# Room for routed rows by rank, and the ranks' room looked up with a matmul

## The chip, the cores and the metric

The kernel runs on one core of a Trainium2 chip. The metric is device time in microseconds (us), the median over runs of the whole kernel. Engines: TensorE (PE; PEld is its weight load), VectorE (DVE), ScalarE (ACT), GpSimd (POOL) and SyncE (SP), which issues most DMAs.

## The reference

One transformer layer in float32 on x of 2 x 1024 tokens by 256 channels: a layer norm and grouped attention (16 heads, 4 key/value heads, head size 16, rotary positions), added to x; then a layer norm and a mixture of experts, added as well. What matters here is the second half, for 2048 tokens:

```python
shared = silu(gu[:, :704]) * gu[:, 704:] @ se_down_w.T * sigmoid(x @ shared_gate_w.T)
probs = softmax(x @ gate_w.T)               # 60 experts
weights, sel = top_k(probs, 4)
for e in range(60):                          # w13[e]: 352 x 256, w2[e]: 256 x 176
    h = silu(x @ w13[e].T[:, :176]) * (x @ w13[e].T[:, 176:])
    sparse += cw[:, e, None] * (h @ w2[e].T)
out = x + shared + sparse
```

Only four experts of sixty have a weight for a token, so 8192 rows (token, expert) need an expert's work, about 137 each and unevenly spread.

## The kernel before, in words

Stages, in order of time: attention over 128 steps (0 to about 360 us), in the gaps of which tokens are routed; the first half of the shared expert, on which the end of routing is laid (to about 418 us); the routed experts (to about 614 us); the second half of the shared expert, on which the gathers of the routed results are laid; the output.

**Routing** (`route`) finds each token's four experts and a slot for each. Tokens go to DRAM (`xg`) by indirect DMA (L739): each expert has 2048 slots there, of which the first `CAP` = 208 were filled at the start with empty rows (L163). An empty row carries the token number `NONE` = 1e6, so its result is dropped by the bounds check of the scatter back.

**Ranks.** The program is fixed before the counts are known. So `count` and `ranks` order the experts by their number of rows on the chip, and the program's r-th expert is whichever has rank r; its number is read into a register from `byrank` (L810, L972). The list `CAPS` gives the room, in rows, with which rank r is worked on: 208 for 6 ranks, 192 for 4, 176 for 8, 160 for 10, 144 for 8, 128 for 24, together 9,248. `ranks` makes `slotid` (L813, L818: slot numbers of the first and second tile of each rank) and `caps` (L824 to L832: the room of each expert, built up in five steps of two operations). From `caps` and the counts comes `nblk` (L847): how many blocks of 128 rows lie beyond an expert's room. If any does (L1278), a loop over all 60 experts works off the rest, block by block (`over_block`).

**The expert stage.** Rooms over 128 are worked in two tiles of half the room each, others in one tile (`tile_of`, L1164). For each rank in the order `turn_of` (L959, which spreads the sizes evenly):

- `bring` loads 624 KB of weights into one of eight buffers (L984), `rows_of` loads the rows from `xg` (L1172), both on SP's queue;
- `turned` transposes the rows on PE (L1182, one per tile and half of the channels) and DVE copies the result to `xT` (L1188);
- `up` has six matmuls on PE with as many columns as the room (L917), SiLU on ACT (L924, L926) and products on DVE (L925, L927) into `hbuf`;
- `second` lets `place` (L947) compute where each row's result goes (`dst`, L952 and L956 on DVE), multiplies by the second weights (L1200: two matmuls of 256 columns for each tile), copies on ACT (`ys`, L1207) and scatters from POOL (L933, one indirect DMA for each tile).

The order on every engine of this stage but POOL is written out by hand: `up` of expert k, `turned` of k+2, `second` of k-1, then the row load of k+4 and the weight load of k+7. In the shared expert's first half the order is also by hand: after each step of matmuls (L863, L885) a piece of routing or ranking follows.

Of the kernel before, what the change touches and what calls it, by code (L numbers as in the profile page):

```python
# [8 lines left out]
F32 = mybir.dt.float32  # L9
# [3 lines left out]
ALU = mybir.AluOpType  # L13
# [3 lines left out]
P = 128  # L17
# [8 lines left out]
E, I = 60, 176  # L26
# [7 lines left out]
FB = 512  # L34
RB = 4

CAPS = [208] * 6 + [192] * 4 + [176] * 8 + [160] * 10 + [144] * 8 + [128] * 24
CAP = max(CAPS)
SP = CAP // 2
ES = NT * P  # L40
OB = -(-(ES - min(CAPS)) // P)
SLT, TOK = C, C + TOPK
XA = 4
WA = 8
XR = C + 16
# [2 lines left out]
NONE = 1e6  # L48
# [3 lines left out]
def attention_moe_kernel(  # L52
# [9 lines left out]
    ws2: bass.AP,  # L62
    rope: bass.AP,
    odd: bass.AP,
    tri: bass.AP,
    out: bass.AP,
):
    nc = tc.nc
# [9 lines left out]
    const = ctx.enter_context(tc.tile_pool(name="const", bufs=1, side="left"))  # L78
# [5 lines left out]
    ident = const.tile([P, P], F32, name="ident")  # L84
# [5 lines left out]
    xg = dram.tile([E * ES + 2 * P, XR], F32, name="xg")  # L90
# [47 lines left out]
    wout_sb = ends_of.tile([P, G // 2, C], F32, name="wout_sb")  # L138
    nc.sync.dma_start(wout_sb, wout)
    nc.sync.dma_start(wgate_sb, wgate.rearrange("(c p) n -> p c n", p=P))  # L140
    tri_sb = const.tile([P, P], F32, name="tri_sb")
    nc.sync.dma_start(tri_sb, tri)
    for a, b in ((RB, TPB), (TPB, NT)):
        nc.sync.dma_start(
            xT_sb[:, :, a * P : b * P], xtr[:, a * P : b * P].rearrange("(c p) n -> p c n", p=P)
        )
        nc.sync.dma_start(acc[:, a:b, :], xt[:, a:b, :])
# [13 lines left out]
    for e in range(E):  # L161
        rows = xg[e * ES : e * ES + CAP, :].rearrange("(t p) c -> p t c", p=SP)
# [3 lines left out]
    for i in range(TOPK * NT // 2):  # L166
        rows = yt[2 * i * P : 2 * (i + 1) * P, :].rearrange("(t p) c -> p t c", p=P)
# [4 lines left out]
    slotid = const.tile([P, E, 2], F32, name="slotid")  # L172
    keyrow = const.tile([P, E], F32, name="keyrow")
    keycol = const.tile([E, 1], F32, name="keycol")
    down = const.tile([E, E], F32, name="down")
    expno = const.tile([E, P], F32, name="expno")
    slot1 = const.tile([P, 1], F32, name="slot1")
    rowno = const.tile([P, OB], F32, name="rowno")
    kplace = const.tile([P, TOPK], F32, name="kplace")
    tokno = const.tile([P, NT], F32, name="tokno")  # L180
    for t, pattern, first, by_row in (

        (base, [[ES, E]], 1, 0),

        (keyrow, [[-1, E]], E, 0),
        (keycol, [[0, 1]], E, -1),
        (down, [[-1, E]], E - 1, 0),
        (expno, [[0, P]], 0, 1),
        (slot1, [[0, 1]], 1, 1),
        (rowno, [[P, OB]], 0, 1),  # L190
        (kplace, [[NT * P, TOPK]], 0, 0),
        (tokno, [[P, NT]], 0, 1),
    ):
        nc.gpsimd.iota(
            t,
            pattern,
            base=first,
            channel_multiplier=by_row,
            allow_small_or_imprecise_dtypes=True,
        )  # L200
    tri_b = const.tile([P, P], BF16, name="tri_b")
    nc.gpsimd.tensor_copy(tri_b, tri_sb)
    ones_b = const.tile([P, P], BF16, name="ones_b")
    nc.gpsimd.memset(ones_b, 1.0)
    ones_f = const.tile([E, P], F32, name="ones_f")
# [17 lines left out]
    start = const.tile([P, E], F32, name="start")  # L223
# [579 lines left out]
    def ranks(bank):  # L803

        who = bank(2 * E, "who")
        nc.tensor.matmul(who[:, 0:E], lhsT=expno, rhs=key["has"], start=True, stop=True)
        nc.tensor.matmul(
            who[:, E : 2 * E], lhsT=ones_f[0:E, :], rhs=key["ahead_of"], start=True, stop=True
        )
        nc.vector.tensor_copy(byrank, who[0:1, 0:E])  # L810
        rank = rk.tile([P, E], F32, name="rank")
        nc.vector.tensor_copy(rank, who[:, E : 2 * E])
        nc.vector.tensor_scalar(slotid[:, :, 0], who[:, 0:E], ES, slot1, ALU.mult, ALU.add)  # L813
        r0 = 0
        for cap in sorted(set(CAPS), reverse=True):
            r1 = r0 + CAPS.count(cap)
            if cap > P:
                nc.vector.tensor_scalar_add(  # L818
                    slotid[:, r0:r1, 1], slotid[:, r0:r1, 0], cap // 2
                )  # L820
            r0 = r1
        yield
        caps = rk.tile([P, E], F32, name="caps")
        nc.vector.memset(caps, float(min(CAPS)))  # L824
        for r in range(1, E):
            if CAPS[r] < CAPS[r - 1]:

                step = rk.tile([P, E], F32, name=f"step{r}")
                nc.vector.tensor_scalar(
                    step, rank, r - 0.5, CAPS[r - 1] - CAPS[r], ALU.is_lt, ALU.mult  # L830
                )
                nc.vector.tensor_add(caps, caps, step)  # L832
        yield
        nc.vector.tensor_sub(over, cnt, caps)
        nc.vector.tensor_add(start, caps, base)
        nc.vector.tensor_copy(cap0, caps[0:1, :])
        more = rk.tile([1, E, OB], F32, name="more_b")
        nc.vector.tensor_tensor(
            more,
            over[0:1, :, None].to_broadcast([1, E, OB]),  # L840
            rowno[0:1, None, :].to_broadcast([1, E, OB]),
            ALU.is_gt,
        )
        blks = rk.tile([1, E + 1], F32, name="blks")
        nc.vector.tensor_reduce(blks[:, 0:E], more, AX.X, ALU.add)
        nc.vector.tensor_reduce(blks[:, E : E + 1], blks[:, 0:E], AX.X, ALU.max)
        nc.vector.tensor_copy(nblk, blks)  # L847
# [96 lines left out]
        tc.add_to_no_dep_group("back", s.ins)  # L944
        scattered.append(s)

    def place(dst, rows, me):  # L947

        n = rows.shape[0]
        k0 = small.tile([n, 1], F32, tag="k0", name="k0")  # L950
        hit = small.tile([n, TOPK], F32, tag="wh", name="wh")
        nc.vector.scalar_tensor_tensor(  # L952
            hit, rows[:, SLT : SLT + TOPK], me, kplace[0:n, :], ALU.is_equal, ALU.mult,
            accum_out=k0,
        )
        nc.vector.tensor_add(dst, k0, rows[:, TOK : TOK + 1])  # L956


    turn_of = [  # L959
        r for _, r in sorted(  # L960
            ((k + 0.5) / CAPS.count(cap), CAPS.index(cap) + k)
            for cap in set(CAPS)
            for k in range(CAPS.count(cap))
        )
    ]
    ws = []
# [29 lines left out]
    with tc.manual_schedule(engines={mybir.EngineType.PE}), ExitStack() as both:  # L996
# [17 lines left out]
        behind = [(0, late)]  # L1014
# [148 lines left out]

        def tile_of(cap):  # L1164

            return (cap // 2, 2) if cap > P else (cap, 1)

        def rows_of(r):
            rows, n = tile_of(CAPS[r])
            no = expert_at(r)  # L1170
            xe = ew.tile([P, 2, XR], F32, tag="xe", bufs=XA + 3, name=f"xe{r}")[0:rows, 0:n, :]
            nc.sync.dma_start(  # L1172
                xe, xg[bass.ds(no * ES, CAPS[r]), :].rearrange("(t p) c -> p t c", p=rows)
            )
            return xe

        def turned(r, xe):
            rows, n = tile_of(CAPS[r])
            tp = ps_x.tile([P, CC, CAP], F32, tag="tpe", name=f"tpe{r}")[:, :, 0 : CAPS[r]]
            for t in range(n):  # L1180
                for c in range(CC):
                    nc.tensor.transpose(  # L1182
                        tp[:, c, t * rows : (t + 1) * rows],
                        xe[:, t, c * P : (c + 1) * P],
                        ident[0:rows, 0:rows],
                    )
            xT = ew.tile([P, CC, CAP], F32, tag="xT", name=f"xT{r}")[:, :, 0 : CAPS[r]]
            nc.vector.tensor_copy(xT, tp)  # L1188
            return xT

        def second(r, w, h, xe):
            rows, n = tile_of(CAPS[r])
            dst = ew.tile([P, 2], I32, tag="dst", name=f"dst{r}")[0:rows, :]
            for t in range(n):
                place(dst[:, t : t + 1], xe[:, t, :], slotid[0:rows, r, t : t + 1])
            po = ps_y.tile([P, 2, C], F32, tag="ye", name=f"ye{r}")[0:rows, 0:n, :]
            ys = ew.tile([P, 2, C], F32, tag="ys", name=f"ys{r}")[0:rows, 0:n, :]
            for t in range(n):
                for k in range(2):
                    nc.tensor.matmul(  # L1200
                        po[:, t, :],
                        lhsT=h[:, k, t * rows : (t + 1) * rows],
                        rhs=w[:, CC * W1C + k * C : CC * W1C + (k + 1) * C],
                        start=k == 0,
                        stop=k == 1,
                    )
            nc.scalar.copy(ys, po)  # L1207
            for t in range(n):
                send_back(ys[:, t, :], dst[:, t : t + 1])
# [113 lines left out]
def _laid_out(inputs):  # L1323
# [20 lines left out]
    for m in range(NC2):  # L1344
# [10 lines left out]
    rope = np.concatenate([cos, cos, -sin, sin], 1).astype(np.float32)  # L1355
    q = a["q_kernel"].reshape(C, NKV, G // 2, 2 * H).transpose(0, 2, 1, 3).reshape(C, NH * H)
    wout = a["out_kernel"].reshape(NKV, G // 2, 2 * H, C).transpose(0, 2, 1, 3)
    return {
        "x": a["x"],
        "xtr": a["x"].reshape(B * T, C).T,  # L1360
# [5 lines left out]
        "ws2": ws2,  # L1366
        "rope": rope.reshape(TPB, P, 2 * H).transpose(1, 0, 2),
        "odd": (np.arange(P) // H % 2).astype(np.int32)[:, None],
        "tri": np.triu(np.ones((P, P), np.float32), 1),
    }  # L1370


# [20 lines left out]
```

## Time and profile before

| | us |
|---|---|
| median of 3 runs (677.0 to 678.4) | 678.12 |
| the profiled execution | 678.74 |
| its span, first to last instruction | 676.9 |
| PE busy in the span | 663.9 |
| first row transpose of the expert stage, start | 417.85 |
| last pass of the expert stage, end | 613.22 |
| first matmul after it (L863), start | 614.55 |
| last matmul (L885), end | 673.3 |

A row of the profile names the line, the engine, the operation and its tiles, out<-in, with the shape and the number of instructions. A busy PE is not a PE at its peak, since matmuls are pipelined; the spacing of their starts says more than the length of one. A wait names the engine and line that waited, then the one that ended the wait, then total us, times and the longest.

### The profile page before, as it was taken

What the parts mean: (1) busy time and instruction counts of PE and PEld (TensorE: products, weight loads), DVE (VectorE), ACT (ScalarE), POOL (GpSimd) and SP (SyncE); (2) the same over time, 40 slices, a digit from 0 to 9 for tenths busy, and PEclk for the clock granted to TensorE, in tenths of its full rate; (3) what the DMA queues carried; (4) which work ended last, traced back from release to release, by engine and by line L of the source; (5) the groups of instructions that cost most, each with busy time, mean ns of one, the idle gap of its engine ahead of it and who ended that gap; (6) DMA issues with size and microseconds to landing.
All of it is one profiled execution on the core that took longest, in us unless ns stands there. A gap on an engine that the chain in (4) does not pass through costs nothing. (4 is left out here: it accounts for less than half of the span.)

```text
span 676.9 us, 12425 instructions
## 1 busy us (share of the span) xinstructions
PE 663.9 (98%) x4156; PEld 375.9 (56%) x4157; DVE 361.7 (53%) x1404; ACT 355.7 (53%) x503; POOL 185.7 (27%) x250
## 2 busy tenths in 40 slices
PE   8999999999999999999999998999999999999997
PEld 7432332442224223233235477898998989885466
DVE  5653755427154376556657755444444434543984
ACT  3678778768986787877862400333333333332210
POOL 4020020011000034533135451444444454543000
PEclk9999999999999999999999999999999999999999
DMA  8999930002100011211011084799989899933951
GB/s 274 294 285 298 333 124 1 1 1 92 42 1 1 0 43 42 75 51 50 9 51 66 34 317 163 252 292 296 298 284 307 286 287 293 299 90 113 309 178 48
DMA packets 64275, 106.33 MB, mean 157 GB/s; under 512 B 7417, under 2 KB 51209, under 8 KB 64210
## 3 DMA queue, kind: packets, MB, share of 16 engines
q1 hardware_dynamic: 55010, 86.57, 39.6%
q0 software_dynamic: 7680, 17.32, 7.4%
q10 hardware_dynamic: 1520, 1.64, 0.7%
q8 instruction: 33, 0.54, 0.3%
q14 instruction: 32, 0.26, 0.1%
HBM read 64.13 MB, written 42.45 MB: 157 GB/s over the span
## 5 line engine op out<-in xcount | busy, mean ns | idle before, releaser
L545 PE MATMUL sc<-qT,kT 32*128 32x512 f32 x1024 | 160.3, 639 | 0.8 <-DVE vaug L335 0.5
L560 ACT ACTIVATE ex<-sc,rqk 128x1024 f32<-128x1024 f32 x128 | 134.2, 1111 | 36.8 <-PE sc L545 35.1
L1068 PE MATMUL av<-ex,vaug 128*32 128x512 f32 x1024 | 137.3, 604 | 2.6 <-DVE den L586 1.8
L560 ACT ACTIVATE ex<-sc 128x1024 f32<-128x1024 f32 x128 | 124.1, 1022 | 28.2 <-PE sc L545 24.6
L933 POOL DMA_INDIRECT yt<-ys,dst x96 | 92.8, 966 | 115.2 <-ACT ys L1207 67.5
L545 PEld LDWEIGHTS sc<-qT,kT 32*128 32x128 f32 x1024 | 52.7, 183 | 109.1 <-issue 67.5
L1200 PE MATMUL ye<-w,hbuf 128*128 128x256 f32 (+5 forms) x384 | 93.3, 381 | 0.0
L739 POOL DMA_INDIRECT xg<-xs,idx x64 | 63.3, 989 | 100.7 <-DVE idx L734 73.5
L863 PE MATMUL sg<-x2T,ws_sb 128*128 128x512 f32 x176 | 78.1, 596 | 1.2 <-ACTq L1278 1.2
L917 PE MATMUL gua<-xT,w 128*128 128x128 f32 (+5 forms) x480 | 73.2, 295 | 0.5 <-DVE xT L1188 0.5
L917 PEld LDWEIGHTS gua<-xT,w 128*128 128x128 f32 x480 | 70.1, 191 | 4.8 <-issue 0.6
L1207 ACT COPY ys<-ye 128x256 f32<-128x256 f32 (+5 forms) x60 | 29.9, 499 | 73.0 <-PE ye L1200 47.4
L1200 PEld LDWEIGHTS ye<-w,hbuf 128*128 128x128 f32 (+5 forms) x384 | 58.9, 164 | 14.5
L1068 PEld LDWEIGHTS av<-ex,vaug 128*32 128x32 f32 x1024 | 20.4, 107 | 79.0 <-issue 66.1
L925 DVE TENSOR_TENSOR hbuf<-hbuf,gua 128x128 f32<-128x128 f32 (+5 forms) x60 | 18.9, 315 | 85.0 <-ACT hbuf L924 45.9
L863 PEld LDWEIGHTS sg<-x2T,ws_sb 128*128 128x128 f32 x176 | 32.6, 190 | 38.9 <-issue 35.5
L924 ACT ACTIVATE hbuf<-gua 128x128 f32<-128x128 f32 (+5 forms) x60 | 17.9, 299 | 64.7 <-PE gua L917 41.8
L506 POOL TENSOR_TENSOR t<-u,rope_sb 128x128 f32<-128x128 f32 x24 | 12.4, 545 | 129.5 <-DVE u L492 129.5
L873 ACT ACTIVATE hs<-sg 128x512 f32<-128x512 f32 (+1 forms) x24 | 14.3, 596 | 59.0 <-PE sg L863 56.7
L885 PE MATMUL so<-ws_sb,hs 128*128 128x256 f32 x192 | 42.5, 381 | 1.5 <-DVE acc L893 1.5
L917 PE MATMUL gub<-xT,w 128*112 128x128 f32 (+5 forms) x240 | 41.2, 294 | 0.0
L885 PEld LDWEIGHTS so<-ws_sb,hs 128*128 128x128 f32 x192 | 36.2, 190 | 8.2 <-DVE acc L893 2.2
(184 smaller groups left out, 663.1 us busy)
## 6 DMA issues: line engine op xcount, KB each, us to landing
w<-in_wexp_dram SPq DMA_DIRECT2D x60, 624.0 KB
xg<-void SPq DMA_DIRECT2D x60, 221.0 KB
yt<-zero SPq DMA_DIRECT2D x32, 256.0 KB
got<-yt SPq DMA_DIRECT2D x16, 512.0 KB
xe<-xg SPq DMA_DIRECT2D x24, 136.0 KB
xe<-xg SPq DMA_DIRECT2D x10, 170.0 KB
yt<-ys,dst POOLq DMA_INDIRECT x96
xe<-xg SPq DMA_DIRECT2D x8, 187.0 KB
```

The lines of the kernel that those rows point to most:

```text
L545: nc.tensor.matmul(sc[:, gg, :], lhsT=kT[b][r : r + 32, jj, s0 : s0 + P], rhs=qT[b][r : r + 32, jp, t0 : t0 + QB], start=True, stop=True,)
L560: nc.scalar.activation(ex, sc, AF.Exp, scale=rqk[:, 1, i : i + 1] if b == 0 else 1.0)
L739: s = nc.gpsimd.indirect_dma_start(out=xg[:, :], out_offset=bass.IndirectOffsetOnAxis(ap=at_, axis=0), in_=xs[:, i, :], in_offset=None, bo ...
L863: nc.tensor.matmul(p, lhsT=ws1_sb[:, c, c0 : c0 + P], rhs=x2T[:, c, n * FB : (n + 1) * FB], start=c == 0, stop=c == CC - 1,)
L885: nc.tensor.matmul(po, lhsT=hs[:, m, t * P : (t + 1) * P], rhs=ws2_sb[:, m, :], start=m == 0, stop=m == NC2 - 1,)
L917: nc.tensor.matmul(ps[part][0:m, 0:n], lhsT=w[:, c * W1C + c0 : c * W1C + c0 + m], rhs=xT[:, c, 0:n], start=c == 0, stop=c == CC - 1,)
L924: nc.scalar.activation(h[:, 0, 0:n], ps["ga"][:, 0:n], AF.Silu)
L925: nc.vector.tensor_mul(h[:, 0, 0:n], h[:, 0, 0:n], ps["ua"][:, 0:n])
L933: s = nc.gpsimd.indirect_dma_start(out=yt[:, :], out_offset=bass.IndirectOffsetOnAxis(ap=at, axis=0), in_=y, in_offset=None, bounds_check= ...
L1068: nc.tensor.matmul(av[32 * g : 32 * g + 32, :], lhsT=vaug[:, b * TPB + s, g, H * jj : H * jj + 32], rhs=es[g // 2][:, g % 2, :], start=s == 0,
L1200: nc.tensor.matmul(po[:, t, :], lhsT=h[:, k, t * rows : (t + 1) * rows], rhs=w[:, CC * W1C + k * C : CC * W1C + (k + 1) * C], start=k == 0 ...
L1207: nc.scalar.copy(ys, po)
```

## The change

Four things are done. The list of rooms has a step for nearly every rank; 24 ranks keep 128, and 36 still have two tiles. The height of the first tile is half the room, rounded up to a multiple of eight (`first_of`); the second tile is loaded with the same height, but only the rows within the room are transposed, and the slots beyond it get `NONE` added to their destination (`behind`, from a table that is loaded with `tri`). The room of each expert is found by a comparison of ranks with a row number and a matmul (`has_room`, `rooms`), with a small table `room` that is loaded at the start, and the second slot numbers by one addition of a table. The order of the ranks is made of every fourth rank of the 36, mixed with the 24.

```diff
-CAPS = [208] * 6 + [192] * 4 + [176] * 8 + [160] * 10 + [144] * 8 + [128] * 24
+CAPS = [208, 208, 208, 200, 192, 186, 182, 178, 176, 174, 172, 170, 168, 166, 164, 162, 160, 158]
+CAPS += [156, 154, 154, 152, 150, 148, 146, 146, 144, 142, 142, 140, 140, 138, 138, 136, 136, 134]
+CAPS += [128] * 24
...
+def first_of(cap):
+
+    return -(-cap // 16) * 8
...
-    tri_sb = const.tile([P, P], F32, name="tri_sb")
+    tri_sb = const.tile([P, P + 2 * E], F32, name="tri_sb")
     nc.sync.dma_start(tri_sb, tri)
+    room_sb = const.tile([E, 1], F32, name="room_sb")
+    nc.sync.dma_start(room_sb, room)
...
+        (rankno, [[0, 1]], 0, 1),
...
-        r0 = 0
-        for cap in sorted(set(CAPS), reverse=True):
-            r1 = r0 + CAPS.count(cap)
-            if cap > P:
-                nc.vector.tensor_scalar_add(
-                    slotid[:, r0:r1, 1], slotid[:, r0:r1, 0], cap // 2
-                )
-            r0 = r1
+        nc.vector.tensor_add(slotid[:, :, 1], slotid[:, :, 0], tri_sb[:, P : P + E])
         yield
+
+        has_room = rk.tile([E, E], F32, name="has_room")
+        nc.vector.tensor_scalar(
+            has_room, rank[0:E, :], rankno, room_sb, ALU.is_equal, ALU.mult
+        )
+        rooms = bank(E, "rooms")
+        nc.tensor.matmul(rooms, lhsT=ones_f[0:E, :], rhs=has_room, start=True, stop=True)
         caps = rk.tile([P, E], F32, name="caps")
-        nc.vector.memset(caps, float(min(CAPS)))
-        for r in range(1, E):
-            if CAPS[r] < CAPS[r - 1]:
-
-                step = rk.tile([P, E], F32, name=f"step{r}")
-                nc.vector.tensor_scalar(
-                    step, rank, r - 0.5, CAPS[r - 1] - CAPS[r], ALU.is_lt, ALU.mult
-                )
-                nc.vector.tensor_add(caps, caps, step)
+        nc.vector.tensor_copy(caps, rooms)
         yield
...
-        nc.vector.tensor_add(dst, k0, rows[:, TOK : TOK + 1])
+        nc.vector.scalar_tensor_tensor(
+            dst, k0, behind, rows[:, TOK : TOK + 1], ALU.add, ALU.add
+        )
...
+    n2 = sum(cap > P for cap in CAPS)
+    by_4 = [r for k in range(4) for r in range(k, n2, 4)]
     turn_of = [
         r for _, r in sorted(
-            ((k + 0.5) / CAPS.count(cap), CAPS.index(cap) + k)
-            for cap in set(CAPS)
-            for k in range(CAPS.count(cap))
+            [((k + 0.5) / n2, r) for k, r in enumerate(by_4)]
+            + [((k + 0.5) / (E - n2), n2 + k) for k in range(E - n2)]
         )
     ]
...
-            return (cap // 2, 2) if cap > P else (cap, 1)
+            return (first_of(cap), 2) if cap > P else (cap, 1)
...
-                xe, xg[bass.ds(no * ES, CAPS[r]), :].rearrange("(t p) c -> p t c", p=rows)
+                xe, xg[bass.ds(no * ES, n * rows), :].rearrange("(t p) c -> p t c", p=rows)
...
+                m = min(rows, CAPS[r] - t * rows)
                 for c in range(CC):
                     nc.tensor.transpose(
-                        tp[:, c, t * rows : (t + 1) * rows],
-                        xe[:, t, c * P : (c + 1) * P],
-                        ident[0:rows, 0:rows],
+                        tp[:, c, t * rows : t * rows + m],
+                        xe[0:m, t, c * P : (c + 1) * P],
+                        ident[0:m, 0:m],
                     )
...
-                place(dst[:, t : t + 1], xe[:, t, :], slotid[0:rows, r, t : t + 1])
+                behind = tri_sb[0:rows, P + E + r : P + E + r + 1] if t else 0.0
+                place(dst[:, t : t + 1], xe[:, t, :], slotid[0:rows, r, t : t + 1], behind)
```

The order of ranks starts with rooms 128, 160, 176, 144, 128, 208 before and with 208, 128, 192, 128, 176, 168 after; it ends with 144, 128, 160, 128 before and with 128, 138, 128, 134 after.

More of the change, by code (lines that the diff above doesn't have):

```diff
@@ L65, in attention_moe_kernel @@
     tri: bass.AP,
+    room: bass.AP,
     out: bass.AP,
@@ L176, in attention_moe_kernel @@
     expno = const.tile([E, P], F32, name="expno")
+    rankno = const.tile([E, 1], F32, name="rankno")
     slot1 = const.tile([P, 1], F32, name="slot1")
@@ L201, in attention_moe_kernel @@
     tri_b = const.tile([P, P], BF16, name="tri_b")
-    nc.gpsimd.tensor_copy(tri_b, tri_sb)
+    nc.gpsimd.tensor_copy(tri_b, tri_sb[:, 0:P])
     ones_b = const.tile([P, P], BF16, name="ones_b")
@@ L945, in send_back, with place @@
         scattered.append(s)
-    def place(dst, rows, me):
+    def place(dst, rows, me, behind=0.0):
         n = rows.shape[0]
@@ L1357, in _laid_out @@
     wout = a["out_kernel"].reshape(NKV, G // 2, 2 * H, C).transpose(0, 2, 1, 3)
+    half = np.tile([first_of(cap) if cap > P else 0 for cap in CAPS], (P, 1)).astype(np.float32)
+    behind = np.where(np.arange(P)[:, None] + half < np.array(CAPS), 0, NONE).astype(np.float32)
     return {
@@ L1368, in _laid_out @@
         "odd": (np.arange(P) // H % 2).astype(np.int32)[:, None],
-        "tri": np.triu(np.ones((P, P), np.float32), 1),
+        "tri": np.concatenate([np.triu(np.ones((P, P), np.float32), 1), half, behind], 1),
+        "room": np.array(CAPS, np.float32)[:, None],
     }
```

## The prediction

> **What bounds the kernel now.** I began with the page's busy shares and slices, to find which engine and which stretch the change can move.
>
> ```profile
> PE 663.9 (98%) x4156; PEld 375.9 (56%) x4157; DVE 361.7 (53%) x1404; ACT 355.7 (53%) x503; POOL 185.7 (27%) x250
> ...
> PE   8999999999999999999999998999999999999997
> ...
> DMA  8999930002100011211011084799989899933951
> ```
>
> TensorE (PE) is busy nearly all the time. The expert stage (slices 26 to 36) has two candidates for the bound: PE and, at 9 tenths, DMA. To see whether PE's rows are work or latency I read its timeline near the end of that stage (start, length, row; the length contains latency, so I use differences of starts):
>
> ```profile
> 606.81 1.25 PE L917 MATMUL gua<-xT,w 128*128 128x160 f32 x8
> ...
> 607.90 0.71 PE L917 MATMUL gub<-xT,w 128*112 128x160 f32 x4
> ...
> 608.44 1.03 PE L1200 MATMUL ye<-w,hbuf 128*128 128x256 f32 x4
> ...
> 609.31 1.05 PE L917 MATMUL gua<-xT,w 128*128 128x128 f32 x8
> ```
>
> The program has 4 gua and 2 gub matmuls per expert; the trace has twice as many, so each fp32 matmul is two passes. 160 columns: (607.90 - 606.81)/8 = 136 ns a pass; 256 columns: (609.31 - 608.44)/4 = 217 ns. In the last stage 96 passes of 256 columns take 20.73 us, so 0.844 ns a column. Transposes have one pass each. Check over the stage, with the 9,248 columns that the rooms before add up to: up 12 x 9,248 x 0.844 = 93.7 us, transposes 2 x 9,248 x 0.844 = 15.6, down 384 x 216 ns = 82.9, together 192.2. The stage runs from the first transpose at 417.85 to 613.22, 195.4 us. So 98% of it is columns through PE.
>
> Is DMA a second bound? The waits of the SP queue, from 410 to 615 us, say what holds back weight loads:
>
> ```profile
> SPq L984 <- PE ye L1200: 37.6, 29, 6.7
> SPq L1172 <- DMA xg<-xs,idx: 11.9, 1, 11.9
> SPq L984 <- PE gua L917: 5.3, 3, 1.9
> ```
>
> Weight loads (L984) wait for PE to release one of eight buffers, not for transfers under way; the one wait for a DMA is that of the first row load, for the routing's scatters. From 380 to 620 us PE itself waits for:
>
> ```profile
> PE so L885 <- DVE acc L893: 1.5, 1, 1.5
> PE sg L863 <- ACTq L1278: 1.2, 1, 1.2
> PE gua L917 <- DVE xT L1188: 0.5, 1, 0.5
> ```
>
> All three lie at the stage's edges. After it PE runs without a gap through L863 and L885 to 673.3, so time saved in the stage should reach the end.
>
> [...] here loads are busy 17.8 to 18.3 of 20 us in the stage's full slices[...]. [...]
>
> **The change, part by part.**
>
> 1. Rooms by rank. They add up to 8,900, 348 fewer. Up passes: 348 x 12; transposes, cut to the room: 348 x 2. 348 x 14 x 0.844 ns = **-4.1 us** on PE. With the slope of the gua rows (286 ns at 144, 339 at 208: 0.83) it is -4.0. The 36 experts with two tiles stay 36, so the 384 down passes of 256 columns stay. A few second tiles have 62 to 66 columns, 52 to 56 ns a pass; [...] under 0.1 us in all. ACT and VectorE (DVE) work on these columns shrinks too, but isn't on the path: ACT is busy about 6.6 and DVE 9.2 of 20 us.
>
> 2. Ranks made anew. L818 (five, 0.46 us) and L824 to L832 (390.92 to 392.84) go. In their place DVE has an add (0.22), has_room (as L795, 0.24) and a copy (0.20). Nothing on the path needs them: byrank (L810), for which SP waits, is ahead of them, and nblk is read after the stage. But has_room feeds a new matmul in PE's order, between the two halves of an up step. It costs PE half of what the two "who" matmuls took (389.11 to 389.69), **+0.3 us**. Does it wait? PE reaches it at 389.69 + 4 x 0.432 = 391.4. DVE ends slotid at 390.4, then add, an idx (0.15) and has_room: 391.1. No wait, with 0.3 us to spare. Were DVE later, all of PE, then ACT and DVE through hs, would stand behind it; I allow 0 to 1.0. Zero, because PE's 1.5 us wait for L893 before the stage may swallow it. DVE's copy of rooms then waits for PE until about 391.8; behind it stand an idx and hs, which ran at 392.76 and 393.50.
>
> 3. The new order starts with a room of 208, not 128. Its copy to xT (0.41 us for 256 elements, 0.51 for 352, so 0.58 for 416) stands before the first gua: **+0.2 us**. Its rows are 221 KB in place of 136; the first two loads together are 357 KB, before 306. All six first loads land within 412.2 to 418.1, and at some 200 KB per us the second is late by 0.25; the first transpose is at 417.85. The order ends with two tiles, not one: before the branch at L1278 ACT copies 72x512 (0.58) and not 128x256 (0.37): **+0.2 us**. The two scatters behind the branch stay two; gathers start at 620 and aren't waited for by PE.
>
> 4. Nothing for the rest, with its cover. dst becomes a scalar_tensor_tensor (0.14 to 0.15 as L734, before 0.16), 96 of them on DVE, which is half idle. Scatters stay 96 on POOL, row loads 60 on SP; rows loaded fall from 9,248 to 9,120. At the start, rankno (0.13 on POOL) lies ahead of a 3.8 us wait for tri_sb. That load grows from 64 to 124 KB, 0.2 us at 284 GB/s, and POOL's next needed work (L402) has 1.8 us of idle ahead of it. The load of room_sb goes in SP's queue ahead of xT_sb tiles 4 to 7: each load there waits for one some eight back, so they go at up to 8.06 and not 5.84. Their first matmul is at 23.2.
>
> Sum: -4.1 + 0.3 + 0.2 + 0.2 = -3.4 us. Against the profiled execution's 678.74 (span 676.9) it gives 675.3. That execution is 0.6 above the median of 678.12, so the forecast median is **674.7**. Beside the sum, PE's 1.5 us wait comes from L893 starting late at 407.55 and 411.87 for no reason that the trace names; it may vanish or double: +/-1.5.
>
> **The rivals.** DMA becomes the bound. Its share is 0.88 to 0.94, and PE asks 2% faster. If the stage stays at 195.4, the three extras remain: 678.8. For it: the share. Against: the waits of SP above, and seven weight buffers of lead, over 20 us. About 6 in 100.
>
> New widths are dear. 29 rooms are no multiple of 16, a kind of fp32 pass that the trace doesn't show. They are 29 x 12 = 348 up passes; 9.8 ns more per pass eats the 3.4 us, and slower by 0.2% needs 13.7. Between 5 and 20 ns: 676.4 to 681.7. Against: 72, 88 and 104 column transposes follow the line (72: 0.25 us for four). Below nothing it cannot go. About 6 in 100.
>
> The other side: rows overflow. The reference's routing of these inputs gives, ranked, counts of 200, 185, 183, 177, ...; all fit, but the least spare room falls from 3 rows to 1 (rank 14: 163 of 164). Two more rows there and the loop at L1278 runs over all 60 experts. [...] It decides from the first row over. The before trace has 60 weight loads, none in that loop. About 3 in 100.
>
> **How the numbers follow.** The main case has 85 in 100, at 674.7, from 672.8 (wait gone) to 676.6 (wait doubled, matmul stalled). It and a little of two rivals give faster 0.87; lost gain gives same 0.07; dear widths and overflow give slower 0.06. The bound is 0.2%, 1.4 us, about what these measurements tell apart. The range is the main case's.
>
> **What would show it.** Right: the stage lasts some 191.5 us, up passes of 154 or 186 columns start 130 or 157 ns apart, PE has no new wait inside, SP still waits for PE. Wrong: PE waits for w or xe (first rival), gua passes off the line (second), a 61st weight load (third), or a PE wait at the rooms matmul (step 2).

## The result, and the profile after

The changed kernel takes **674.32 us** (median of 6 runs, 673.72 to 675.77) against 678.29 (6 runs, 677.0 to 678.74) for the kernel before: a ratio of **0.9946, 95% interval 0.9933 to 0.9958**. The forecast was 674.7. The profiled execution of the changed kernel took 674.28 us with a span of 672.5; the one before had 678.74 and 676.9.

The busy shares and slices of the page after:

```profile
PE 661.4 (98%) x4158; PEld 373.0 (55%) x4159; DVE 361.0 (54%) x1391; ACT 355.4 (53%) x503; POOL 185.5 (28%) x251
...
PE   8999999999999999999999999999999999999997
...
DMA  8999950002100001111011076699999999934951
```

PE has 2.5 us less to do and is still busy everywhere. DMA now shows a 9 in all nine slices from the 27th to the 35th, in which the experts' weights come in; before, two of these had an 8. The timeline of PE near the end of that stage (start, length, row):

```profile
605.23 1.08 PE L924 MATMUL gua<-xT,w 128*128 128x134 f32 x8
606.14 0.62 PE L924 MATMUL gub<-xT,w 128*112 128x134 f32 x4
606.60 2.75 PE L1213 MATMUL ye<-w,hbuf 128*128 128x256 f32 x12
610.23 7.13 PE L870 MATMUL sg<-x2T,ws_sb 128*128 128x512 f32 x16 [0.89 <-ACTq L1291]
```

Eight passes of 134 columns start (606.14 - 605.23)/8 = 114 ns apart, 0.85 ns a column: on the line, though 134 is no multiple of 16. In the same trace the other widths from 136 to 208 have 0.845 to 0.852 ns a column, but for the very first expert. From 380 to 620 us PE waits for two things only:

```profile
PE sg L870 <- ACTq L1291: 0.9, 1, 0.9
PE gua L924 <- DVE xT L1200: 0.6, 1, 0.6
```

Of the three waits of before, the one for the sums (1.5 us, then `PE so L885 <- DVE acc L893`) is gone. SP's queue, from 410 to 615 us:

```profile
SPq L995 <- PE ye L1213: 70.3, 52, 6.5
...
SPq L1183 <- DMA xg<-xs,idx: 12.4, 1, 12.4
```

Weight loads still wait for PE, 52 times where it was 29, so in this execution transfers kept up.

Where the 4.4 us of span came from is read by cutting PE's timeline at the same places in every execution. The columns: from the first `sc` matmul of the attention to the first of the two `who` matmuls; to the first `so` matmul of the shared expert's first half (L892, L885 before), whose results VectorE sums; to the first row transpose; to the first `gua`; from there to the end of the last `ye`; the gap at the branch. The last stage after it is 58.75 us in both. (Here the stage ends with the last `ye` row, at 613.38 us before; the table of times ahead of the prediction has 613.22, which is the start of that last pass and one spacing of 0.217; passes overlap in the records, one of these has a length of 0.38.)

| us | sc to who | who to so | so to transposes | to gua | expert stage | branch gap |
|---|---|---|---|---|---|---|
| before | 369.29 | 5.83 | 22.91 | 1.16 | 194.37 | 1.17 |
| after | 369.58 | 6.39 | 20.72 | 1.33 | 191.33 | 0.88 |
| difference | +0.29 | +0.56 | -2.19 | +0.17 | -3.04 | -0.29 |

The first `sc` started 0.18 later; over all the traces its start lies between 19.70 and 20.80 us, so that is not the change's. The stage gives most, but 2.2 us come from a stretch in which the change saves PE no work: the right total was put together from pieces of which not all were foreseen.

### The profile page after: what moved, and what is told of

Same layout as the page of the kernel before. It is cut to its first block, busy times and chain, and to the rows that moved or that the text cites. A ratio compares the mean times of both kernels' runs of the same rounds, so it can differ in the third digit from the quotient of the medians.

```text
span 672.5 us, 12420 instructions
## 1 busy us (share of the span) xinstructions
PE 661.4 (98%) x4158; PEld 373.0 (55%) x4159; DVE 361.0 (54%) x1391; ACT 355.4 (53%) x503; POOL 185.5 (28%) x251
## 5 line engine op out<-in xcount | busy, mean ns | idle before, releaser
L924 PE MATMUL gua<-xT,w 128*128 128x128 f32 (+28 forms) x480 | 70.9, 291 | 0.6 <-DVE xT L1200 0.6
L924 PEld LDWEIGHTS gua<-xT,w 128*128 128x128 f32 x480 | 68.4, 191 | 5.1 <-issue 0.8
L932 DVE TENSOR_TENSOR hbuf<-hbuf,gua 128x128 f32<-128x128 f32 (+28 forms) x60 | 18.5, 309 | 86.4 <-ACT hbuf L931 84.7
L931 ACT ACTIVATE hbuf<-gua 128x128 f32<-128x128 f32 (+28 forms) x60 | 17.7, 294 | 51.4 <-PE gua L924 51.4
L892 PE MATMUL so<-ws_sb,hs 128*128 128x256 f32 x192 | 41.8, 379 | 0.0
L924 PE MATMUL gub<-xT,w 128*112 128x128 f32 (+28 forms) x240 | 40.1, 289 | 0.0
L892 PEld LDWEIGHTS so<-ws_sb,hs 128*128 128x128 f32 x192 | 36.5, 190 | 5.8 <-issue 1.0
```

The costliest lines, as they stand in the source:

```text
L892: nc.tensor.matmul(po, lhsT=hs[:, m, t * P : (t + 1) * P], rhs=ws2_sb[:, m, :], start=m == 0, stop=m == NC2 - 1,)
L924: nc.tensor.matmul(ps[part][0:m, 0:n], lhsT=w[:, c * W1C + c0 : c * W1C + c0 + m], rhs=xT[:, c, 0:n], start=c == 0, stop=c == CC - 1,)
L931: nc.scalar.activation(h[:, 0, 0:n], ps["ga"][:, 0:n], AF.Silu)
L932: nc.vector.tensor_mul(h[:, 0, 0:n], h[:, 0, 0:n], ps["ua"][:, 0:n])
```

## The experiments

They ran in three groups, each on a chip of its own. The kernel before had medians of 679.35, 679.35 and 679.88 us there; each ratio is to the runs of the same group. before_again, pad13, oldrooms and rooms138 are the first group; after_again, w4, xa6 and short_second the second; the others the third. Runs made once have no interval, and are read by their stretches. Line numbers in variants can be shifted by a few.

### The kernel before once more, and thirteen idle instructions

**before_again** is the kernel before, unaltered. **pad13** is the changed kernel with thirteen more VectorE operations at the start:

```diff
+    spare = const.tile([P, 13], F32, name="spare")
+    for f in range(13):
+        nc.vector.memset(spare[:, f : f + 1], 0.0)
```

> The kernel before, profiled once more. In its first profile PE waited 1.5 us at L885 for L893 (VectorE), which started 2.2 and 3.7 us after its matmuls; in the changed kernel that wait is gone and the stretch from the first L885 pass to the first row transpose fell from 22.9 to 20.7 us. If the wait belongs to this program, it is here again (stretch 22 to 23.5 us). If it is chance of one execution, the stretch is 20.7 to 21.2 us here, and up to 2.2 us of the 4.4 us between the two profiled spans are not due to the change. Also: the first scores (L545) started at 19.82; repeat within 0.1 us if the 0.2 us of the changed kernel's later start is real.

> The changed kernel with 13 small VectorE memsets at the start, where VectorE is idle: they restore the number of VectorE instructions ahead of the shared expert's end (the change took 13 away). If the late L893 of before hangs on where in VectorE's program the stretch lies (a fetch of instructions is seen at 407.5 us in both profiles), the wait comes back: the stretch of 96 L892 passes up to the first transpose takes 22 us and more, the span is 674 to 675. If it hangs on the operations that the change took away, it stays at 20.7 us and the span at 672.5 +/- 0.5.

before_again took 678.57 us, its stage 194.42 and "so to transposes" 22.07. So the kernel before keeps its long stretch, though its wait is 0.6 us this time. pad13 took 677.81, and its 22.72 us before the transposes have the wait of 1.5 us again. That alone would look like an effect of where instructions lie; the next run of the unpadded kernel takes that reading away.

### The changed kernel once more, twice

> The changed kernel, timed and profiled once more beside before. Its first profile lacked the late start of the shared expert's fourth and fifth sums (L900) that before and three variants show, 1.5 to 2.1 us on the path, and any wait for row loads, of which three variants have one of 0.4 to 1.1 us. If the program itself is free of both, the ratio is 0.9946 again and the stretch from the first L892 pass to the first transpose is 20.7 us. If both belong to the chip or the execution, the ratio is 0.996 to 0.997, the stretch 22 to 23 us, and one wait for xe stands in the expert stage.

> The changed kernel, unaltered, on the same chip, so that the stretches of the other three can be compared with it: stage 191.3 to 192.1 us, depending on whether PE waits for the rows of one expert of 208; 6.39 us from 'who' to the sums; the late fourth and fifth sum (L900) as in all executions but one.

after_again: 677.43 us (7 runs), **ratio 0.9964 (0.9952 to 0.9975)**. after_third: 678.70 in one run. Both have the wait for the sums. The timeline of VectorE (L900) and PE (L892) in after_again:

```profile
403.64 0.48 DVE L900 SCALAR_TENSOR_TENSOR acc<-so,sg,acc 128x256 f32<-128x256 f32 x1 [1.97 <-issue]
408.20 0.48 DVE L900 SCALAR_TENSOR_TENSOR acc<-so,sg,acc 128x256 f32<-128x256 f32 x1 [3.94 <-remote]
...
412.51 0.48 DVE L900 SCALAR_TENSOR_TENSOR acc<-so,sg,acc 128x256 f32<-128x256 f32 x1 [3.69 <-PE so L892]
...
413.05 3.23 PE L892 MATMUL so<-ws_sb,hs 128*128 128x256 f32 x13 [1.45 <-DVE acc L900]
```

and in the first execution of the same kernel:

```profile
403.94 0.48 DVE L900 SCALAR_TENSOR_TENSOR acc<-so,sg,acc 128x256 f32<-128x256 f32 x1 [1.97 <-PE so L892]
406.53 0.48 DVE L900 SCALAR_TENSOR_TENSOR acc<-so,sg,acc 128x256 f32<-128x256 f32 x1 [1.97 <-PE so L892]
409.12 0.48 DVE L900 SCALAR_TENSOR_TENSOR acc<-so,sg,acc 128x256 f32<-128x256 f32 x1 [1.97 <-PE so L892]
411.87 0.48 DVE L900 SCALAR_TENSOR_TENSOR acc<-so,sg,acc 128x256 f32<-128x256 f32 x1
```

One kernel, two executions: in the first one a sum every 2.59 us, as PE delivers; in the new one two sums that follow after 4.56 and 4.31 us, so 2.0 and 1.7 us late. Since the same program does both, the 2.19 us of the table can't be counted as the change's.

Nor is it the luck of one execution. All six runs of the changed kernel in the first comparison took 673.72 to 675.77 us, all seven here 676.34 to 678.09. The medians are 3.1 us apart; those of the kernel before in the same two comparisons are 1.1 apart (678.29 and 679.35). So the absence seems to go with the occasion (the session, or the chip, which the record doesn't name for the first one), and not with one execution. The kernel before had the wait in the first comparison, in the one run of its six that was profiled; whether the change has a part in its absence from the changed kernel there is not shown.

In the stage the new executions have another wait, for the rows of an expert of 208 rows (two tiles of 104), not seen in the first. PE in after_third:

```profile
558.69 0.60 PE L924 MATMUL gub<-xT,w 128*112 128x128 f32 x4
560.26 0.54 PE L1194 MATMUL tpe<-ident,xe 104*128 104x104 f32 x4 [0.97 <-DMA xe<-xg]
```

It is 0.7 us in after_again (stage 192.08) and 1.0 in after_third, where 0.7 more stood at 479.57 with no releaser named (stage 193.24).

### Old rooms, looked up the new way (oldrooms)

```diff
+CAPS = [208] * 6 + [192] * 4 + [176] * 8 + [160] * 10 + [144] * 8 + [128] * 24
-CAPS = [208, 208, 208, 200, ...]
-    n2 = ...      # and the order of ranks of the kernel before
```

> The changed kernel with the six classes of room and the order of ranks of before: only the room lookup by a matmul, the two tables and the masked destination remain. Theory: the 348 columns are the gain, about 3.5 us net inside the expert stage, and the ranks made anew cost PE 0.5 us at the rooms matmul. Then the stage (first transpose to last second matmul) is 195.4 us again, and the time is before +0.5, less up to 2.2 if the wait for L893 goes with the removed operations: 676.3 to 679. Rival: a good part of the gain is the ladder's removal: then 674 to 676.

679.72 us (20 runs), **ratio 1.0006 (0.9999 to 1.0013)**; the stage is 194.85 us, of which 0.4 is a wait for rows, "who to so" is 6.39 and the branch gap 0.88. So the lookup by matmul, without smaller rooms, gains nothing that can be measured, and the gain is that of the columns. The gap at the branch is the new, shorter one although this order ends with a single tile, as before.

### Does a width cost? The last rooms at 138 (rooms138)

After the changed kernel, three groups of transposes stood out, those of the ranks with rooms of 136, 136 and 134, whose second tiles have 64, 64 and 62 rows. PE in the first execution after, a group with tiles of 72 and 68 rows, then one with 72 and 64:

```profile
546.45 0.42 PE L1194 MATMUL tpe<-ident,xe 72*128 72x72 f32 x4
546.70 1.90 PE L1213 MATMUL ye<-w,hbuf 128*80 128x256 f32 x8
...
553.14 0.56 PE L1194 MATMUL tpe<-ident,xe 72*128 72x72 f32 x4
553.63 1.13 PE L1213 MATMUL ye<-w,hbuf 128*128 128x256 f32 x4
```

From the first transpose to the next operation: 0.25 us, and 0.49. The passes themselves hardly differ (groups by form; the number before the last bar is the mean length of one in ns):

```profile
L1194 PE MATMUL tpe<-ident,xe 66*128 66x66 f32 x8 | 1.1, 223 | 0.0
...
L1194 PE MATMUL tpe<-ident,xe 64*128 64x64 f32 x4 | 0.7, 247 | 0.0
...
L1194 PE MATMUL tpe<-ident,xe 62*128 62x62 f32 x2 | 0.3, 248 | 0.0
```

The other 0.2 us lie between operations, and the four `ye` passes that follow these three groups take 0.97 us to the start of the next operation, where they take 0.90 to 0.92 behind the other groups of two tiles. The experiment takes these rooms away:

```diff
-CAPS += [..., 138, 138, 136, 136, 134]
+CAPS += [..., 138, 138, 138, 138, 138]
```

> The changed kernel with ranks 33, 34 and 35 given 138 rows (before: 136, 136, 134), so that their second tiles transpose 66 rows and not 64, 64 and 62. In the changed kernel those three groups of four transposes took 0.48 to 0.51 us, where 66 to 72 rows take 0.25. Theory: transposes of at most 64 rows cost a switch, 0.24 us a group, whatever their columns; then all three groups take 0.25, and with 8 columns more (8 x 14 x 0.844 ns = 0.09 us) the stage is 0.6 us shorter. Rival: the weight load outlasts such narrow passes; [...] the groups stay above 0.4 us or fall by less than 0.03. The time is the same within what can be told (0.1%).

677.15 us (20 runs), ratio 0.9967 (0.9958 to 0.9977). All groups of this kind now take 0.25 to 0.27 us. The transposes of the stage together, each counted from its start to that of the next operation without waits, fall from 15.75 us in the first execution after to 15.09, and the `ye` passes counted alike from 84.00 to 83.85. But PE waits 1.1 us for rows of the 104-row tile, and so the stage is 191.96: the total shows nothing, the pieces do.

### Twenty short second tiles (short_second)

```diff
-    return -(-cap // 16) * 8
+    return 96 if cap <= 160 else -(-cap // 16) * 8
```

> The changed kernel with a first tile of 96 rows for the 20 ranks with rooms of 134 to 160, so that all their second tiles have 38 to 64 rows; columns, matmuls and passes stay, 20 row loads grow to 192 rows. Theory of the 64-row switch: 17 more groups of transposes cost 0.24 us each, so the stage (first up pass to last second matmul) grows by about 4.1 us, to 195 or 196. [...] Under the theory no group of second tiles of 66 rows or more is above 0.4 us.

681.67 us in one run. The stage is 196.40 us, 4.3 more than in after_again. By pieces, the transposes take 4.3 us more (15.71 to 20.01) and the `ye` passes behind them 1.05 more (84.01 to 85.06); the 0.7 us wait for rows of after_again is absent, and the up passes are 0.3 shorter. PE's timeline of it, second tiles of 44 and 40 rows first and last, a single tile of 128 between:

```profile
552.25 0.58 PE L1194 MATMUL tpe<-ident,xe 96*128 96x96 f32 x4
552.75 1.97 PE L1213 MATMUL ye<-w,hbuf 128*96 128x256 f32 x8
...
555.88 0.38 PE L1194 MATMUL tpe<-ident,xe 128*128 128x128 f32 x2
556.10 1.89 PE L1213 MATMUL ye<-w,hbuf 128*96 128x256 f32 x8
...
559.26 0.57 PE L1194 MATMUL tpe<-ident,xe 96*128 96x96 f32 x4
559.76 1.13 PE L1213 MATMUL ye<-w,hbuf 128*128 128x256 f32 x4
```

Twenty groups take 0.50 to 0.53 us, whether the second tile has 38 rows or 64. Seventeen more than in after_again make 4.3 / 17 = 0.25 us each in the group, and 1.05 / 17 = 0.06 in the `ye` passes that follow, so 0.31 in all: a fixed price, with a border between 64 and 66 rows.

### Fewer early weight loads (w4)

```diff
-            for k in range(WA):
+            for k in range(WA // 2):
...
+            for k in range(WA // 2, WA):
+                bring(k)      # after the first row loads
```

> The changed kernel with only four of the first eight weight loads ahead of the scatters' end, the other four after the first four row loads. Eight loads and the scatters keep the DMA engines full (415 to 430 GB/s) from about 396 to 409 us, and the late L900 starts at 407.5 to 408.7, just then. Theory: VectorE waits there for something that comes through those DMA engines; with half of the loads gone the lateness is gone: the stretch from the first L892 pass to the first transpose is 20.7 to 21.2 us where the changed kernel beside it has 22 to 23, and the time is 1 to 2 us shorter. Rival: L900 waits for an order of semaphores, not for DMA: the stretch stays, and the time is within 0.5 us of the changed kernel's, or longer if the fifth weights come late.

677.62 us, ratio 0.9967 (0.9952 to 0.9982). The late sums are still there (22.73 us before the transposes, a wait of 1.6), and PE waits 1.3 us for rows in the stage. The same four microseconds in the first execution after, in after_again and in w4 (length, then busy and number for PE, PEld, DVE, ACT and POOL, then the granted clock, the DMA share and GB/s):

```profile
404.00:408.00 4.00, 4.00 (x20) 3.54 (x19) 1.18 (x6) 0.00 (x0) 3.08 (x4) 1.00 1.03 422
```

```profile
404.00:408.00 4.00, 4.00 (x21) 3.51 (x20) 0.26 (x3) 0.00 (x0) 3.08 (x4) 1.00 1.03 422
```

```profile
404.00:408.00 4.00, 4.00 (x20) 3.54 (x19) 1.21 (x6) 0.00 (x0) 3.08 (x4) 1.00 0.38 124
```

The first has full DMA engines and no late sum. w4 has them at 0.38 here, and still its fourth sum is 0.5 us late and its fifth comes 5.7 us after that. So full DMA engines are neither needed for the lateness nor enough for it.

### Rows two experts earlier (xa6)

```diff
-XA = 4
+XA = 6
```

> The changed kernel with row loads six experts ahead in place of four (nine buffers, not seven). Theory: PE's wait for xe at the 46th expert is a matter of lead, since a row load goes out only behind the weight load ahead of it in SP's queue; with two more experts of lead (about 6 us) no wait for xe is left, the stretch from the first up pass to the last second matmul is 191.3 us, as in the profile without the wait, and the time 0 to 1 us shorter than the changed kernel's. Rival: DMA as a whole is short of bandwidth; then the wait stays or moves to w, and the stage is as long as before.

676.00 us (4 runs), ratio 0.9947 (0.9931 to 0.9964). The stage is 190.99, against 192.08 of after_again in the same group, and has no wait for rows. Of these 1.09 us, 0.69 are the wait that is gone, and 0.34 lie in two steps of up passes beside it. In total the time falls by 1.4 us; the intervals of the two ratios overlap, but all four runs (675.78 to 676.09) lie below all seven of after_again (676.34 to 678.09).

### The matmul for rooms over 128 rows (k128)

```diff
-    ones_f = const.tile([E, P], F32, name="ones_f")     # rankno, room_sb alike
+    ones_f = const.tile([P, P], F32, name="ones_f")
...
-        nc.tensor.matmul(rooms, lhsT=ones_f[0:E, :], rhs=has_room, start=True, stop=True)
+        nc.tensor.matmul(rooms, lhsT=ones_f, rhs=has_room, start=True, stop=True)
```

> The changed kernel with has_room, ones_f, rankno and the table of rooms over 128 rows instead of 60, and nothing else: the rooms matmul contracts over 128 rows. Theory (the switch to 64 rows or fewer): the time from the 'who' matmuls to the second half's sums falls from 6.39 to about 6.15 us; 'who' itself keeps its cost. Rival (the matmul costs PE by where it stands between two halves of a step, or by its two passes): 6.39 stays. The rest as in the changed kernel.

"who to so" is 6.06, not 6.39 us: contracting over 60 rows among matmuls of 128 made up 0.33 of the 0.56 us that the matmul cost. That is near the 0.31 of a short group of transposes. The time, 678.10 in one run, is not compared with anything finer than that.

### All three (best)

xa6, rooms138 and k128 together.

> The changed kernel with three edits: rows loaded six experts ahead in place of four; rooms of 138 for the last five ranks over 128, so that no second tile has 66 or fewer rows; has_room, ones_f, rankno and the table of rooms over 128 rows instead of 60, so that the rooms matmul contracts over 128 rows. Theory (a contraction over 64 rows or fewer between others of 128 costs PE a switch of about 0.24 us a group; PE waits for rows only through a short lead): no group of row transposes takes over 0.42 us, the stage lasts 190.3 to 190.6 us from the first gua to the end of the last ye (xa6 190.99, rooms138 191.96), and the time from the 'who' matmuls to the second half's sums falls from 6.39 to about 6.15 us, as only 'who' still contracts over few rows. Whole: 0.7 to 0.9 us below xa6, ratio to the kernel before 0.993 to 0.9945. Rival (the transposes cost by their shape, rooms by where it stands): stage 191.0 or more, 6.39 stays, ratio 0.9947 or above.

**675.18 us (6 runs), ratio 0.9934 (0.9922 to 0.9947)**, the lowest ratio of all. Its PE around the rooms matmul, and below it that of the first execution after:

```profile
390.57 1.98 PE L870 MATMUL sg<-x2T,ws_sb 128*128 128x512 f32 x4
392.39 0.33 PE L837 MATMUL rooms<-has_room,ones_f 128*128 128x60 f32 x2
392.56 3.66 PE L870 MATMUL sg<-x2T,ws_sb 128*128 128x512 f32 x8
```

```profile
390.16 1.98 PE L870 MATMUL sg<-x2T,ws_sb 128*128 128x512 f32 x4
392.07 0.43 PE L837 MATMUL rooms<-has_room,ones_f 60*128 60x60 f32 x2
392.43 3.70 PE L870 MATMUL sg<-x2T,ws_sb 128*128 128x512 f32 x8
```

From the four sg passes to the next sg: 1.99 us with 128 rows, 2.27 with 60. The stage is 190.68 and the transposes in it 14.96 us, 0.71 less than in xa6 for three groups. That the stage is 0.1 longer than expected goes with a small wait of its own (`ye` for `hbuf`, 0.25 us at 510.24). Against the changed kernel the ratios point to about 1 to 3 parts in a thousand; it was timed beside it only in single executions (675.2 and 678.7).

### The old ladder with the new rooms (ladder)

```diff
-        nc.vector.tensor_scalar(has_room, ...)
-        nc.tensor.matmul(rooms, ...)
-        nc.vector.tensor_copy(caps, rooms)
+        nc.vector.memset(caps, float(min(CAPS)))
+        for r in range(1, E):
+            if CAPS[r] < CAPS[r - 1]:
+                ...      # step and add, as in the kernel before; slot numbers too
```

> The changed kernel with the kernel before's way to the rooms (a step of two VectorE operations for each drop in the list of rooms, and one addition of slot numbers for each size) in place of has_room, the rooms matmul and the one addition. The list of rooms stays the new one, so about 29 steps and 29 additions take the place of 5 and 5. Theory: these some 87 operations of 0.14 to 0.24 us stand on VectorE ahead of hs (L882), which the second half of the shared expert waits for: of some 15 us more VectorE work 8 to 13 reach PE as a wait, the time becomes 8 to 13 us longer than that of the changed kernel, and the matmul for 0.56 us is what makes fine rooms affordable. Rival: VectorE's idle time before L893 covers them, at most 1 us longer.

686.22 us in one run, 7.5 more than after_third. The edit brings back both ladders, of rooms and of slot numbers. PE's waits from 392 to 425 us, then stretches of 4 us (columns as in w4):

```profile
PE so L900 <- DVE acc L908: 7.6, 2, 7.2
```

```profile
398.00:402.00 4.00, 2.95 (x14) 2.26 (x12) 3.62 (x24) 0.00 (x0) 0.00 (x0) 1.00 1.02 410
402.00:406.00 4.00, 0.00 (x0) 0.00 (x0) 3.86 (x14) 0.00 (x0) 0.97 (x1) 0.70 1.03 426
406.00:410.00 4.00, 1.83 (x4) 1.52 (x5) 2.65 (x12) 0.00 (x0) 2.30 (x3) 0.50 0.45 178
410.00:414.00 4.00, 4.00 (x11) 3.18 (x10) 0.30 (x1) 0.00 (x0) 3.09 (x4) 0.52 0.36 118
414.00:418.00 4.00, 4.00 (x21) 3.51 (x20) 0.94 (x6) 0.00 (x0) 3.09 (x4) 1.00 0.34 119
```

VectorE is nearly full while PE stands for 7.2 us, and then PE works with a granted clock of 0.5 for some 5.5 us: 11 passes in 4 us where it later does 21. So the wait is 7.6 us, the clock takes some 2.7 more (half of 5.5), and the wait of 1.5 for late sums and the rooms matmul (0.56) are saved: 8.2 against the 8.3 that PE's stretches up to the transposes show. Both the wait and the total lie just below the 8 to 13 us that were expected, and the total comes as near as it does by a clock term that wasn't foreseen.

## Why the prediction was right, and where it wasn't

**The bound (right).** PE's columns carry the stage. The old rooms with everything else new give 1.0006; the up passes keep 0.85 ns a column at every new width, so "new widths are dear" has fallen for them.

**Step 1, -4.1 us: mis-sized, -3.0 in the stage.** The up passes fell from 94.99 to 91.59 us, -3.4 where the step says 348 x 12 x 0.844 = -3.5. The rest is in the transposes, -0.6 expected and +0.2 measured (15.53 to 15.75 us), and in the `ye` passes, nothing expected and +0.15 measured (83.85 to 84.00). The term that failed is "under 0.1 us in all" for second tiles of 62 to 66 rows. It was the author's estimate, and what it took such a tile's weight loads to cost is shown by no trace. The loads are not what was missing: in the first execution after, those of the transposes take 136 to 142 ns at all heights from 62 to 128 rows, and those of the `ye` passes go by their columns, 150 ns for 80 and 190 for 128. But three groups with 64 rows or fewer cost 0.24 us more each, and 0.06 in the passes behind them, 0.9 together. rooms138 removed that and short_second multiplied it. The runs agree in the border, between 64 and 66 rows, and in a fixed price of 0.31 us for each short group. What the expectations call a switch is this extra time; what the engine does in it no view shows.

**Step 2, +0.3 us: mis-sized, +0.56.** No wait, as forecast: `has_room` ended at 391.42 and `rooms` started at 392.07. The price was taken as half of two "who" matmuls, which stand together; `rooms` stands alone among matmuls of 128 rows. k128 shows that 0.33 us of the price go with its 60 rows.

**Step 3: half right.** The first expert's copy is +0.17 as said (+0.2). The tail before the branch is -0.29 in place of +0.2. oldrooms, which ends with a single tile, also has the shorter gap, so neither the order nor the length of ACT's last copy sets it. The traces show what does: before, that copy starts 0.36 us after the end of the last `ye`; in the first execution after and in oldrooms it starts after 0.08, and this 0.28 is the difference of the gaps. The load for ACT's branch goes out 0.02 us after the copy's start in each, so the copy's length, from which the step took its +0.2, is not on the path. Why the copy starts late before, released by PE's sequencer at L1278, is open.

**Step 4, nothing: nearly.** From the first `sc` to `who` every variant of the changed kernel has 369.54 to 369.58 us, both executions of the kernel before 369.29 and 369.30. That is +0.28 us that no step names. All of it arises at one place in the attention, at 286 us: there ACT pauses for PE after two exponentials, where before it did so after four, and it is the same in the other traces of the changed program that were followed through (after_again, oldrooms, ladder, xa6, pad13). Its cause wasn't tried.

**The side remark on the 1.5 us wait** decided the total. In the first execution after, the wait had vanished, as the remark allowed, for -2.2 us with what hangs on it; in all later traces, of either kernel, a wait of the kind is there (0.4 to 1.6 us). Without it the first difference of the spans would be -3.04 + 0.56 + 0.29 + 0.17 - 0.29 - 0.05 (the end) = -2.4 us where the sum says -3.4. The second comparison has 677.43 - 679.35 = -1.9, with a wait for rows of 0.7 in it. So the forecast median was met because an overestimate of the gain by 1.0 us and the absence of a wait fell together; that is luck. Why the sums come late is open: neither pad13 nor w4 settled it.

The ends of the range were not worked out from the terms either: 674.7 with the wait gone is 673.2, and with the wait doubled and the matmul stalled for its full 1.0 us it is 677.2, where the prediction has 672.8 and 676.6. The measured median lies inside either pair.

**The rivals.** "DMA becomes the bound" did not come as a whole, but in a small form: one or two waits for rows, 0.4 to 1.3 us together, in the later traces of the changed kernel and its variants with rows four experts ahead (all but the slower short_second); with six experts ahead, in xa6 and best, there is none. oldrooms has 0.4 us of it at the old pace of PE, so the faster pace is not its only cause. Its place was not the weights, whose lead the prediction weighed, but the rows, whose lead inside the stage it left out. "Rows overflow" did not occur: there are 60 weight loads, and what the loop would have cost no run shows.

## What to carry to other kernels

Where TensorE is bound by columns, work it off at the width that the data need; in these runs a width that is no multiple of 16 cost nothing by itself (0.845 to 0.852 ns a column), but keep a tile's contraction above 64 rows, or pad it, when its neighbours use more: a short group cost 0.31 us here. Look up a table with a small matmul rather than a ladder of VectorE steps once there are many steps (with the list of five steps it made no difference here, 679.72 us against 679.35; with that of 28 the ladders took 7.5 us more), and give it 128 rows (0.33 us less than with 60). When an engine that sets the pace gets faster, check the lead of every kind of load, the small ones too; and for a change of half a per cent cut the timeline into stretches and repeat it on another occasion, since one total can be right by two errors.

## What the runs showed of the hardware that was not expected

- Two passes with a contraction over 64 rows or fewer, among others that contract over more, cost about 0.25 us beyond their own time, and the passes behind them 0.06 more: groups of four transposes took 0.48 to 0.53 us where the second tile had 38 to 64 rows, 0.25 to 0.27 where it had 66 to 72. Two matmul passes over 60 rows cost 0.33 us more than over 128.
- In a pause of PE of 7.2 us (ladder, 400.95 to 408.17) the granted clock fell to 0.50, which it shows from 404 to 405 us, and it was back at 1.00 some 5.5 us after work had resumed. What was not foreseen is that this wait of 7.2 us drags about 2.7 us more behind it, an estimate from half of those 5.5.
- The same program shows or lacks a wait of 1.5 us, with VectorE sums that start some 2 us late for no reason that the trace names. The one trace without it is of the first comparison; every later one, from three chips, has it or a shorter one, with the DMA engines full or at 0.38.
